# A second Strassen level for four of the seven Q, K and V products, with the sums of x on GpSimd

## The chip, the cores and the metric

The kernel runs on one core of one Trainium2 chip. The metric is the device time of one execution in microseconds (us). The core has five engines with instruction queues of their own: TensorE (PE in the profile, PEld for its weight loads), VectorE (DVE), ScalarE (ACT), GpSimd (POOL) and SyncE (SP), which here only issues DMA transfers. Each queue is worked off in order; engines wait for each other through semaphores.

## The reference, cut to what matters

The program is a small transformer stack on x of shape (8, 512, 1024) in float32. Its first layer is the one that matters here:

```python
qkv = layernorm(x) @ attn_qkvw + attn_qkvb          # (8, 512, 1024) @ (1024, 3072)
q, k, v = split into 32 heads of 32
probs = softmax(q @ k.T / sqrt(32))
ctx = probs @ v
x = x + ctx @ attn_ow + attn_ob                      # (8, 512, 1024) @ (1024, 1024)
```

After it come a dense layer gated by cluster hits, a sigmoid attention, and the dense layer once more. All matrix products are done in float32.

## The kernel before, in words

**Units.** The softmax attention (`softmax_attention`, L421) is a loop over 64 units (L1041). A unit is one batch (of 8) and one group of four heads, 128 columns of Q, K and V. For its four blocks of 128 rows a unit does: scores by rows for the next unit into one PSUM tile `sc` of four banks (`rows_step`, L905), the row maximum by DVE (L906), scores by keys with the maximum subtracted (`keys_step`, L934 and L937, the same single `sc` tile), exp by ScalarE into one of three `pT` buffers (L939), the running sum of `pT` by GpSimd (`sum_step`, L949), and the product with V (`values_step`, L960). `normalize` (L964) divides by the sum and writes `ctxT`.

**Filler.** Everything else that PE has to do is cut into pieces with a weight in us and put into the queue `Filler` (L74). Nine slots of a unit (`between`, L985) each take a share of that queue (`FILLER_SHARES`, L39) between two attention steps. So the order of PE's instructions is written out by hand when the program is built. The pieces come from `project_pieces(n + 2)` (Q, K and V of the unit two ahead), from the output products (`out_products`, L843; `OUT_SHARES` and `LAST_SHARES` say how many of them each unit takes) and from the finished output tiles. All these products go through `product` (L574), so their matmuls are on line L578. Their accumulators are tiles `mm` of one bank from a pool of three (`ps_m`), which the transposes, the denominators and the cluster logits use too.

**Strassen.** From batch 1 on, Q/K and V are computed by one level of Strassen's method in Winograd's form: seven products of half size instead of eight. `LEFT` and `RIGHT` (L139) name the seven operands on the side of x and of the weights. For Q/K of one unit the right-hand columns are Q's and K's, and a product is 4 `product` calls that stream 256 tokens past 128 weight columns. V is done for two units together, with x stationary and 128 weight columns streaming. `gather` (L149) adds each finished product from PSUM into the results: seven DVE adds and two ScalarE copies per set of seven products. `left_sums` (L180) makes the four sums of x of a batch on DVE, 128x1024 each (`left_tasks`, L671). The sums of the weights are made once, on DVE during batch 0, from the weight blocks that batch 0 loads anyway (`sum_weights`, L599), and stored to DRAM by GpSimd's DMA queue. Batch 0 itself uses plain products (`first_pieces`, L617).

**Weights.** A `Stream` (L199) loads weight blocks of 256 KB on SP's queue into six buffers, in the order in which PE will use them (`order`, L464); a block is loaded when the block six before it has been used. The output weights have a stream of their own with six buffers (`OW_BUFS`).

**Small work.** Lists `side` and `slow` hold steps that `between` issues beside the filler: the normalisation of the next batch (`norm_tasks`, L520, its scaling by GpSimd on L558), sums of x, sums of weights.

Of the kernel before, what the change touches and what calls it, by code (L numbers as in the profile page):

```python
# [13 lines left out]
F32 = mybir.dt.float32  # L14
# [8 lines left out]
P = 128  # L23
# [14 lines left out]
W_BUFS, OW_BUFS = 6, 6  # L38
FILLER_SHARES = (0.5, 0.5, 0.6, 1.0, 1.0, 1.0, 0.7, 1.0, 1.0)  # L39

OUT_SHARES = (2, 2, 2, 1)

OUT_SUMS = {0: (0,), 5: (1, 2), 7: (3,)}
LAST_SHARES = {-7: 0, -6: 1, -5: 1, -4: 2, -3: 2, -2: 6, -1: 2}
# [103 lines left out]

def gather(nc, k, acc, ia, ib, ja, jb, bias=(None, None), early=False):  # L149
# [30 lines left out]
def left_sums(nc, a11, a12, a21, a22, s1, s2, s4):  # L180

    tt = nc.vector.tensor_tensor
    steps = [
        partial(tt, s1, a21, a22, ALU.add), partial(tt, s2, s1, a11, ALU.subtract),
        partial(tt, a21, a11, a21, ALU.subtract), partial(tt, s4, a12, s2, ALU.subtract),
    ]
    return dict(A11=a11, A12=a12, A22=a22, S1=s1, S2=s2, S3=a21, S4=s4), steps
# [11 lines left out]
class Stream:  # L199
# [6 lines left out]
    def fill(self, upto):  # L206
        while self.loaded < min(upto, len(self.sources)):
            k = self.loaded
            self.tiles[k] = self.pool.tile(self.shape, F32, tag=self.tag, name=f"{self.tag}_{k}")
            self.nc.sync.dma_start(self.tiles[k], self.sources[k]())  # L210
# [210 lines left out]
def softmax_attention(tc, cst, stage, filler, clusters, pools, dr, late, args):  # L421
# [14 lines left out]
    fixed, ctxp, rpool, npool = outer("a_fixed", 1), outer("a_ctx", 2), outer("a_r", 3), outer("a_n", 1)  # L436
    owpool, csp, xTp, sump = outer("a_ow", OW_BUFS), outer("a_cs", 1), inner("a_xT", 2), inner("a_sum", 1)
    wpool, xpool = inner("a_w", W_BUFS), inner("a_x", 2)
    qkpool, vpool, ptp, tmp = inner("a_qk", 3), inner("a_v", 5), inner("a_pt", 3), inner("a_tmp", 1)
# [9 lines left out]
    xTs, ctxTs, state, lefts = {}, {}, {}, {}  # L449
    units, half = B * NC, NC // 2  # L450

    def quarter(t, g, k):

        return w_view[:, ts(k, half), ts(t * NC + g, P)]

    def weight_source(kind, g, name):

        if name[0] == "T":
            return dr.sums[kind, g, name].rearrange("p (c n) -> p c n", c=half)
        t, g = ((0, g) if name[2] == "1" else (1, g)) if kind == "qk" else (2, 2 * g + int(name[2]) - 1)  # L460
        return quarter(t, g, int(name[1]) - 1)

    V_PARTS = (RIGHT[:4], RIGHT[4:])
    order = []  # L464
    for u in range(NC, units):
        g = u % NC
        order += [("qk", g, RIGHT[k]) for k in EARLY] + [("v", g // 2, name) for name in V_PARTS[g % 2]]
# [11 lines left out]
    used, side, slow, tiles, waiting, ready, held = {"w": 0}, deque(), deque(), deque(), deque(), deque(), []  # L479

    def first_norm():
# [5 lines left out]
        def load(i):  # L487
            pool, tag = (npool, ("n1", "nT")[i % 2]) if i > 1 else (xpool, "x")
# [31 lines left out]
    def norm_tasks(b):  # L520
# [9 lines left out]
        def load(i):  # L530
            st[i] = xpool.tile([P, H], F32, tag="x", name=f"x_{b}_{i}")
# [24 lines left out]
        def apply(k, j):  # L556
# [5 lines left out]
            [partial(load, 0), partial(load, 1)],  # L562
            [partial(turned, k) for k in range(NC // 2)] + [partial(stats, 0), partial(stats, 1)],
            [partial(load, 2), partial(load, 3)],
            [idle] * 3 + [partial(stats, 2), partial(stats, 3)],
            [root, shift, send, idle, spread],
# [13 lines left out]
    first_w = {}  # L580

    def load_first(g, kinds):

        if g >= NC:
            return
        if not first_w:
            first_w["qk"] = ctxp.tile([P, NC, S], F32, tag="ctxT", name="w_first")
        if 2 in kinds:
            wv = rpool.tile([P, H], F32, tag="r", name=f"wv_{g}")
        for t in kinds:  # L590
            for k in range(2):
                at = ts(k, S) if t == 2 else ts((g % 2) * 4 + 2 * t + k, S)
                flat = wv if t == 2 else first_w["qk"].rearrange("p c t -> p (c t)")
                w = first_w[t, g, k] = flat[:, at].rearrange("p (c n) -> p c n", c=half)
                nc.sync.dma_start(w, quarter(t, g, k))
# [1127 lines left out]
```

## Time and profile before

| | |
|---|---|
| runs of the kernel | 3712.62, 3714.6 and 3715.97 us, median 3714.6 |
| the profiled execution | 3715.75 us, span of its instructions 3714.0 us, mean granted clock 0.998 |
| DMA | 598.56 MB, 161 GB/s over the span |
| weight blocks of 256 KB for Q, K and V (`w`) | 252 from the weights, 224 and 112 from stored sums; 2.7 to 3.0 us from issue to landing |
| output weight blocks (`ow`) | 240 from stored sums, 180 from the weights; 3.6 and 3.3 us to landing |

How to read the profile: a row of a group gives line, engine, operation, the tiles written and read, the shapes and the count; then the busy time, the mean duration of one in ns, and the idle time just before them with what ended it. A row of the timeline gives start and duration in us and the number of instructions in the run; durations of matmuls overlap with the next start, so costs are read from start to start. Rows of waits give the total, the number of times and the longest.

### The profile page before, as it was taken

How to read it: one execution, taken by the hardware profiler on the slowest of the kernel's cores; microseconds unless marked ns; L12 is line 12 of the kernel's file. 1: busy time of each engine (PE TensorE's matmuls, PEld its weight loads, DVE VectorE, ACT ScalarE, POOL GpSimd, SP SyncE). 2: the span in 40 equal slices, each digit the busy share in tenths (PEclk: the TensorE clock that was granted, in tenths of full speed). 3: DMA queues.
4: the chain of work that ended last, by engine and by line, in shares of the span. 5: the costliest groups of instructions: out<-in, count | busy, mean ns of one | idle time of the engine just before them, and what ended most of it. 6: DMA issues, size and time to landing. Idle time of an engine off the chain costs nothing.

```text
span 3714.0 us, 76568 instructions
## 1 busy us (share of the span) xinstructions
PE 3677.2 (99%) x32792; PEld 1879.6 (51%) x32792; DVE 2171.2 (58%) x2993; ACT 928.0 (25%) x1017; POOL 1418.9 (38%) x1206
## 2 busy tenths in 40 slices
PE   8999999999999999999999999999999999999999
PEld 4445545545445445455555455534444467774444
DVE  4556555555555555555555555555788845556656
ACT  1222222222222222222222223232111144430000
POOL 2575454454445346345444544442000044530000
PEclk9999999999999999999999999999999999999999
DMA  5345555655655555464565544456566767763332
GB/s 184 106 129 182 143 145 151 183 148 152 185 155 149 169 164 152 143 198 142 149 182 150 151 149 123 122 160 229 158 180 178 184 185 236 222 222 125 133 132 98
DMA packets 728642, 598.56 MB, mean 161 GB/s; under 512 B 322152, under 2 KB 574064, under 8 KB 728304
## 3 DMA queue, kind: packets, MB, share of 16 engines
q1 hardware_dynamic: 701072, 496.40, 47.5%
q0 software_dynamic: 22912, 81.54, 5.6%
q10 hardware_dynamic: 4320, 15.73, 1.0%
q8 instruction: 259, 4.24, 0.5%
q14 instruction: 79, 0.65, 0.1%
HBM read 459.30 MB, written 134.25 MB: 160 GB/s over the span
## 4 chain that ended last, share of the span: by engine, by line
PE 96%; DVE 1%; POOL 1%; issue 1%; DMA 0%; ACT 0%; SPq 0%; POOLq 0%; DVEq 0%; ACTq 0%
PE mm L578 43%; PE dense L1283 21%; PE sc L905 7%; PE av L960 6%; PE sc L937 6%; PE o L1364 4%; PE csc L1345 4%; PE sc L934 2%; PE logitsT L339 2%; PE den L972 1%; PE tp L291 1%; POOL sum L949 0%; PE tpm L578 0%; DMA ow<-o_T 0%; DVE nmax L906 0%
## 5 line engine op out<-in xcount | busy, mean ns | idle before, releaser
L906 DVE TENSOR_REDUCE nmax<-sc 128x4 f32<-128x2048 f32 x256 | 586.5, 2291 | 368.5 <-PE sc L905 365.9
L939 ACT ACTIVATE pT<-sc 128x2048 f32<-128x2048 f32 x256 | 480.7, 1878 | 1113.4 <-PE sc L937 1105.9
L949 POOL TENSOR_TENSOR sum<-sum,pT 128x1024 f32<-128x1024 f32 x256 | 601.1, 2368 | 388.5 <-ACT pT L939 388.4
L949 POOL TENSOR_TENSOR sum<-pT,pT 128x1024 f32<-128x1024 f32 x128 | 309.3, 2438 | 573.9 <-ACT pT L939 547.7
L578 PE MATMUL mm<-xT,w 128*64 128x256 f32 (+1 forms) x3736 | 427.3, 382 | 0.0
L578 PEld LDWEIGHTS mm<-xT,w 128*64 128x64 f32 (+1 forms) x3736 | 241.5, 135 | 202.6 <-issue 44.0
L578 PE MATMUL mm<-s,w 128*32 128x256 f32 (+1 forms) x3672 | 321.0, 381 | 0.0
L905 PE MATMUL sc<-qk,qk 32*64 32x512 f32 x4096 | 285.1, 613 | 0.8 <-ACT pT L939 0.7
L578 PEld LDWEIGHTS mm<-s,w 128*32 128x32 f32 (+1 forms) x3672 | 181.0, 122 | 177.3 <-issue 74.0
L937 PE MATMUL sc<-qk,qk 32*128 32x512 f32 x2048 | 262.9, 587 | 0.0
L156 DVE TENSOR_TENSOR u<-dense,u 128x512 f32<-128x512 f32 x223 | 148.0, 685 | 185.0 <-PE dense L1283 169.6
L578 PE MATMUL mm<-ow,ctxT 128*32 128x512 f32 (+2 forms) x1276 | 249.7, 601 | 2.9 <-DMA ow<-o_T 2.7
L960 PE MATMUL av<-pT,v 128*32 128x512 f32 x2048 | 246.4, 598 | 0.2 <-ACT pT L939 0.2
L1283 PE MATMUL dense<-sum,s 128*128 128x512 f32 x512 | 231.8, 593 | 0.0
L578 PEld LDWEIGHTS mm<-w,xT 128*64 128x64 f32 (+1 forms) x3888 | 197.5, 133 | 62.2 <-issue 48.9
L578 PE MATMUL mm<-w,xT 128*64 128x128 f32 (+1 forms) x3888 | 218.1, 274 | 0.0
L158 DVE SCALAR_TENSOR_TENSOR qk<-mm,qkvb_s,qk 128x256 f32<-128x256 f32 x224 | 107.6, 480 | 155.0 <-PE mm L578 152.3
L156 DVE TENSOR_TENSOR v<-mm,v 128x256 f32<-128x256 f32 x196 | 80.0, 420 | 175.6 <-PE mm L578 174.8
L1283 PE MATMUL dense<-wT_s,dT_b 128*128 128x512 f32 x384 | 171.2, 593 | 0.0
L1283 PE MATMUL dense<-wT_s,dT_a 128*128 128x512 f32 x384 | 171.2, 593 | 0.0
L578 PE MATMUL mm<-ow,c 128*64 128x512 f32 (+2 forms) x864 | 170.0, 596 | 0.3 <-DMA ow<-o_T 0.3
L975 DVE STREAM_TRANSPOSE rden<-den 128x512 f32<-128x512 f32 x64 | 45.9, 717 | 206.6 <-PE den L972 206.6
(236 smaller groups left out, 4772.6 us busy)
## 6 DMA issues: line engine op xcount, KB each, us to landing
w<-in_qkvw SPq DMA_DIRECT2D x252, 256.0 KB, 3.0
ow<-o_T SPq DMA_DIRECT2D x240, 256.0 KB, 3.6
w<-qk_T SPq DMA_DIRECT2D x224, 256.0 KB, 2.8
ow<-in_ow SPq DMA_DIRECT2D x180, 256.0 KB, 3.3
w<-v_T SPq DMA_DIRECT2D x112, 256.0 KB, 2.7
x<-in_x SPq DMA_DIRECT2D x32, 512.0 KB, 4.6
dT_a<-xT SPq DMA_DIRECT2D x32, 512.0 KB, 5.7
x_a<-x SPq DMA_DIRECT2D x32, 512.0 KB, 6.8
```

What stands on the lines that cost most here:

```text
L156: nc.vector.tensor_tensor(out, acc, other, ALU.add)
L158: nc.vector.scalar_tensor_tensor(out, acc, b, other, ALU.add, ALU.add)
L578: nc.tensor.matmul(out[cols], lhsT[:, cols], rhs, **flags)
L905: nc.tensor.matmul(sc[ts(j, P // 2), h, :], st["q"][rows, cols], st["k"][rows, :], start=True, stop=True)
L906: nc.vector.tensor_reduce(st["nmax"][:, qt, :], sc, AX.X, ALU.max, negate=True)
L937: nc.tensor.matmul(sc[:, h, :], st["k"][rows, ts(kt, P)], st["q"][rows, :], start=False, stop=True)
L939: nc.scalar.activation(pT, sc, AF.Exp, scale=SCALE_A)
L949: nc.gpsimd.tensor_tensor(st["sum"][:, h, :], before[:, h, :], st["pT", kt][:, h, :], ALU.add)
L960: nc.tensor.matmul(st["av"][rows, :], st["v"][:, kt, rows], pT[:, h, :], start=(kt == 0), stop=(kt == TPB - 1))
L1283: nc.tensor.matmul(st["acc"], st["left"][LEFT[k]][:, c, :], self.w[RIGHT[k]][:, c, :], start=(c == 0), stop=(c == half - 1),)
L1345: nc.tensor.matmul(sc[:, AT_OFF[i] : AT_OFF[i] + n], k[:, c, ts(i, P)], xT[:, c, i * P :], start=(c == 0), stop=(c == 1),)
L1364: nc.tensor.matmul(acc[:, j - jj, :], at[:, start : start + P], self.v[b * TPB + i][:, cols], start=(i == 0), stop=(i == j),)
```

## The change

Four of the seven products of the first level (the operands numbered 2, 4, 1 and 3 of `LEFT` and `RIGHT`) are themselves done by a second level of the same method. They are taken in pairs, `TWICE = ((2, 4), (1, 3))`; such a pair is called a node here. A node has seven blocks; a block is one weight tile with the operands of both of its products, 4 `product` calls over 128 columns, one accumulator, one `gather`. The three other products ("single" nodes: 0, 5 and 6) stay as they are and are added up by `done`.

- The work is dealt in jobs: Q/K for two units, V for four units. `parts_of` says which part of which job a unit's filler holds: Q/K node pairs in odd units, Q/K singles in even ones; V's first pair when the group's number is 0 modulo 4, the second at 2, the singles at 3. Work for a unit is therefore done up to three units ahead (four at the start of a V job), and starts in unit 4 of batch 0.
- V's single nodes now stream 256 weight columns instead of 128.
- `unit_filler` puts the pieces of output products between the blocks of the doubled nodes; `OUT_SHARES` and `LAST_SHARES` change.
- The sums of x go to GpSimd: per batch four of 1024 elements, four of 512 and eight of 256 (`left_tasks`).
- The sums of weights get a second set of sums (`again`); they load their own operands, and a step of them is issued in each slot with side work, from the scores before unit 0 on. Their results go to DRAM in the block form (`twice`, `once`).
- Batch 0's weights go through the stream too. Pools change: five buffers for Q and K, seven for V, five for output weights, one x buffer; the attention's result lives in six quarter slots (`ctx_s`), with two ScalarE copies at the end (`settle`). The memory for descriptors of GpSimd's DMA queue is set to 4096.

The core of the diff:

```diff
-W_BUFS, OW_BUFS = 6, 6
+W_BUFS, OW_BUFS = 6, 5
+QK_BUFS, V_BUFS, SLOTS = 5, 7, 6
-OUT_SHARES = (2, 2, 2, 1)
+OUT_SHARES = (3, 2, 0, 2)
-LAST_SHARES = {-7: 0, -6: 1, -5: 1, -4: 2, -3: 2, -2: 6, -1: 2}
+LAST_SHARES = {-7: 1, -6: 0, -5: 0, -4: 2, -3: 3, -2: 4, -1: 4}
...
+TWICE = ((2, 4), (1, 3))
+STORED = ("B11", "T3", "B21", "B22", "T1", "T2", "T4")
...
+    def parts_of(u):
+        parts = [("first", u + 2, 0)] if u + 2 < NC else []
+        n = u + 3 if u % 2 else u + 2
+        if NC <= n < units:
+            parts.append(("qk", n, 0 if u % 2 else 1))
+        n = u - u % half + half
+        if n == units:
+            if u % half == 1:
+                parts.append(("v", n - half, 3))
+        elif n >= NC and u % half != 1:
+            last = 4 if n + half < units else 2
+            parts.append(("v", n, (0, None, 1, last)[u % half]))
+        return parts
...
+    def weight_sums(kind, job, c):
...
+        def outer(k):
...
+            st["steps"][k]()
+            if k == 0:
+                once = dr.once[kind, job].rearrange("p (k c n) -> c p k n", k=2, c=2)
+                nc.gpsimd.dma_start(once[c], b11)
+        def again(i, k):
...
+            st["more"][k]()
+            dst = dr.twice[kind, job, i].rearrange("p (m a c n) -> c a p m n", m=7, a=2, c=2)[c]
+            if k == 2:
+                for a in range(2):
+                    nc.gpsimd.dma_start(dst[a, :, 4:], st["z"][:, :, a, :])
+            if k == 3:
+                for a in range(2):
+                    nc.gpsimd.dma_start(dst[a, :, :4], x[:, a].rearrange("p k j n -> p (k j) n"))
...
+        return [load, lambda: None, outers, agains]
...
     def left_tasks(b):
...
+        xT, tt = xTs[b], nc.gpsimd.tensor_tensor
...
+        steps = [
+            partial(tt, e1, b21, b22, ALU.add), partial(tt, e2, e1, b11, ALU.subtract),
+            partial(tt, e3, b11, b21, ALU.subtract), partial(tt, e4, b12, e2, ALU.subtract),
+        ]
...
+        steps += [partial(tt, a21, a11, a21, ALU.subtract), partial(tt, s2, a22, a21, ALU.subtract)]
+        more = [partial(tt, s4, a12, s2, ALU.subtract), partial(tt, s1, s2, a11, ALU.add)]
+        for node, t in ((1, s2), (3, a21)):
...
+            names, own = left_sums(nc.gpsimd, q11, q12, q21, q22, *(e[:, k] for k in range(3)))
...
+        def twice(i, k, at):
+            def go():
...
+                for a in range(2):
+                    for c in range(2):
+                        lhsT, rhs = w[:, a, c, :], left[TWICE[i][a]][k][:, c, :]
+                        if not qk:
+                            lhsT, rhs = rhs, lhsT
+                        product(acc[:, a, :], lhsT, rhs, start=(c == 0), stop=(c == 1))
...
+                gather(nc, k, acc, *(o[j][:, :, m, :] for m in range(2) for j in range(2)), early=True)
+                weights.done(at)
...
+        def done(node, j, acc):
...
+            if node == 0:
+                (ia, ja), (ib, jb) = of(0), of(1)
+                qb = bias(0, j) if qk else None
+                add(ia, acc, qb)
+                add(ib, acc)
+                add(jb, ib)
+                add(ja, jb, qb)
+                return
...
+    def unit_filler(u, products):
+        groups, outs = unit_pieces(u), [piece for product in products for piece in product]
+        many, pieces, at, seen = sum(small for _, small in groups), [], 0, 0
+        for group, small in groups:
+            pieces += group
+            if small:
+                seen += 1
+                upto = len(outs) * seen // many
+                pieces += outs[at:upto]
+                at = upto
+        return weave(pieces, products) if not many else pieces
...
+            if sums:
+                sums.popleft()()
...
-            filler.add(weave(project_pieces(ahead), products), mark=ahead)
...
+        filler.add(unit_filler(n, products), mark=n)
...
-    nc = bacc.Bacc("TRN2", target_bir_lowering=False, num_devices=1)
+    nc = bacc.Bacc("TRN2", target_bir_lowering=False, num_devices=1, dynamic_dma_scratch_size=4096)
```

## The prediction

> **What bounds the kernel now.** I read the page first: its busy times and the chain that ended last. TensorE (PE) is at 99% and the chain is 96% PE. The line to remember is L578, the one matmul line that every projection goes through: 43% of the chain.
>
> ```profile
> PE 3677.2 (99%) x32792; PEld 1879.6 (51%) x32792; DVE 2171.2 (58%) x2993; ACT 928.0 (25%) x1017; POOL 1418.9 (38%) x1206
> PE 96%; DVE 1%; POOL 1%; issue 1%; DMA 0%; ACT 0%; SPq 0%; POOLq 0%; DVEq 0%; ACTq 0%
> ```
>
> An average over the span proves little, so next the busy times by stretch: the 56 units of batches 1 to 7 (second line below), batch 0 before them, the end of the attention after them.
>
> ```profile
> 60.00:277.00 217.00, 215.23 (x2283) 94.44 (x2290) 117.56 (x113) 59.90 (x48) 135.24 (x127) 1.00 0.43 139
> 277.00:2430.00 2153.00, 2150.38 (x25464) 1092.97 (x25455) 1202.37 (x1564) 580.61 (x566) 1019.30 (x722) 1.00 0.54 156
> 2430.00:2600.00 170.00, 157.35 (x1090) 65.35 (x1090) 94.60 (x146) 43.86 (x54) 60.34 (x51) 0.97 0.61 200
> ```
>
> After the time come PE, PEld, DVE, ACT, POOL, then the granted clock, the DMA share and GB/s. In the middle stretch PE idles 2.6 us of 2153 at a granted clock of 1.00, while DVE is at 56%, POOL at 47% and the DMA engines at 54%. So here one us less of PE work is one us less of time, as long as nobody makes PE wait. Only the end has idle PE time (12.7 us).
>
> Third, the timeline of PE gives the price of one `product` (a 128-column stationary operand, issued as two matmuls of 64 columns, each recorded twice: four records).
>
> ```profile
> 1002.63 2.84 PE L578 MATMUL mm<-w,xT 128*64 128x128 f32 x48
> 1005.40 1.11 PE L905 MATMUL sc<-qk,qk 32*64 32x512 f32 x16
> 1006.45 1.95 PE L578 MATMUL mm<-xT,w 128*64 128x256 f32 x16
> 1008.22 0.39 PE L578 MATMUL tpm<-ident_h,parts 128*64 128x128 bf16 x8
> ...
> 1022.70 3.67 PE L578 MATMUL mm<-xT,w 128*64 128x256 f32 x32
> 1026.31 1.11 PE L905 MATMUL sc<-qk,qk 32*64 32x512 f32 x16
> ```
>
> Read from start to start: 12 products over 128 columns take 2.77 us, 0.231 each; 8 over 256 columns take 3.61 us, 0.451 each, and 4 of them 1.77, 0.443 each. Half the columns cost 0.51 of the time, so a second level that halves the moving side does not lose in overhead what it saves.
>
> **What is removed on PE.** Per four units, before: four Q/K groups of 7 x 4 = 28 products over 256 columns (112), and two V jobs of 7 x 8 = 56 over 128 (112). After: each Q/K job of two units has two doubled nodes of 7 blocks x 4 products over 128 columns (56) and three single nodes x 2 columns x 4 over 256 (24); a V job of four units has the same 56 and 24. That is 168 over 128 columns and 72 over 256. Difference: 40 x 0.451 - 56 x 0.231 = 18.0 - 12.9 = 5.1 us per four units, and 14 such groups: 71 us. The attention's own matmuls, the output products and the number of filler slots between them stay, so nothing else moves on PE.
>
> **What is added beside PE.** (a) DVE. Each doubled node gathers as one Strassen level did: 7 adds and 2 ScalarE copies; the three single nodes of a job need the 14 adds that two units need today. Added: 14 adds per Q/K job and 14 per V job, 42 per four units, 588 in all, at the row of L156 (417 to 420 ns): 245 us. The ScalarE copies (372 ns) keep their number. Removed: four sums of x per batch.
>
> ```profile
> L906 DVE TENSOR_REDUCE nmax<-sc 128x4 f32<-128x2048 f32 x256 | 586.5, 2291 | 368.5 <-PE sc L905 365.9 <-PE mm L578 2.5
> L156 DVE TENSOR_TENSOR v<-mm,v 128x256 f32<-128x256 f32 x196 | 80.0, 420 | 175.6 <-PE mm L578 174.8
> L1375 DVE TENSOR_TENSOR s<-xT 128x1024 f32<-128x1024 f32 x7 | 12.5, 1791 | 0.0
> L1375 DVE TENSOR_TENSOR s<-s,xT 128x1024 f32<-128x1024 f32 x7 | 8.6, 1225 | 0.2
> L558 POOL TENSOR_TENSOR xT<-xT,rows 128x1024 f32<-128x1024 f32 x56 | 132.3, 2372 | 0.7
> ```
>
> Those four take 1.79 + 3 x 1.22 = 5.5 us, 38 us over 7 batches. DVE in the middle stretch goes to 1202 + 245 - 38 = 1409 us of some 2082: 68%. It stays under PE, but its bursts grow: a single node 0 ends in four adds (1.7 us), that of V in eight (3.4 us), where one product now ends in two at most.
>
> (b) POOL gets the sums of x: 4 of 1024 elements, 4 of 512 and 8 of 256 a batch. The first at 2.37 us; the others by share of size, 1.2 and 0.6 (an estimate): 19 us a batch, 133 us in all, 1019 to 1152, 55%. They stand ahead of the softmax sums (L949) in POOL's queue, at most 10 us in a unit. Behind these waits the denominator of the next unit, and exp by its three pT buffers. POOL's row of sums is idle 936 us waiting for exp, so the delay is hidden.
>
> (c) Queue of SP: 60 weight blocks of 256 KB per four units instead of 42, 14 x 18 x 256 KB = 66 MB more. At 156 GB/s and a share of 0.54 today that makes about 193 GB/s and 0.67. Six buffers stay. A doubled block lasts 0.9 us on PE, but a unit takes some 37 us for at most 20 of them, so six are 11 us of lead against 2.8 to 3.0 us to landing. SP's own longest row shows the lead: SP waits for PE, not PE for SP. The output weights lose one buffer of six; PE waits 3 us for them now (row "mm<-ow,ctxT"); I add 1 to 4.
>
> ```profile
> SPq L210 <- PE mm L578: 1501.3, 831, 9.1
> PEld mm L578 <- DVE v L156: 44.6, 55, 0.8
> ```
>
> (d) Batch 0. The sums of the weights were 48 adds of 512 elements on DVE (L612, 683 to 908 ns); now 48 of these and 96 of 256, +40 us over nine units of 35 us, at most 3.4 us in one slot and after the row maximum of that slot in the queue; hidden as long as DVE (54% here) has them done before the next maximum, a slot pair of 7 us later. POOL issues 108 stores instead of 48. Its rows are 0.55 us for a plain store and 1.07 us for the one finely cut load (L1405), so +33 to +90 us on a POOL at 62%: up to 9 us a unit. SP's loads for these sums wait for the stores that read the same buffers (landing 4 to 5 us), and weight blocks are queued behind those loads. Cost: 0 to 15 us; no row shows a POOL store with the smaller descriptor memory, so above that lies the case where each issue waits for the landing before (108 x 4.4 us). I take 5.
>
> (e) Work is projected up to three units ahead, so some of the last units' filler moves into batch 0. The last two units get 4 + 4 output products instead of 6 + 2. The idle PE time of 12.7 us lies there; two copies of 128x1024 at 1.23 us (settle) join it. -8 to +8, I take -3.
>
> (f) Waits for the three accumulators. A doubled block fills one in 0.9 us where a single product took 1.8. If two blocks follow the row maximum (2.29 us) and the next slots want the first one's accumulator, PE waits for 2.29 + 0.42 us from the end of the scores. Slots are three pieces or 2.6 us, then keys (1.2 us): mostly covered; in slot one of a unit the first block goes to ScalarE, which is free. The wait row above (weight loads that wait for DVE, 55 times at up to 0.8 us, PE not idle) says that cover is already thin. One wait of 0.5 us in a unit is 28 us, none is 0; I take 8.
>
> **A rule against it.** DVE's first sum of x takes 1791 ns where its like takes 1225, beside POOL's scaling of x. The Trainium skill, "SBUF — State Buffer", section "Who interferes with whom", says that a DVE instruction with two SBUF inputs and a GpSimd one that reads SBUF exclude each other, the later one blocking fully. The change puts more such work on POOL. By it the 168 adds of node 0 with both inputs in SBUF would each wait up to one POOL sum, half of that time on average: by estimate some 1.2 us x 0.55 x 168 = 111 us of DVE, a share of 73%. By the row alone (0.57 us) it is 96 us at the most. Either way the forecast stands.
>
> **The sum.** -71 (PE) + 8 (accumulators) + 2 (output weights) + 5 (batch 0) - 3 (end) = -59. The profiled execution took 3715.75 us (span 3714.0), the median is 3714.6, 1.15 below: 3715.75 - 59 - 1.15 = 3655.6, say 3655.
>
> **Rivals.**
> 1. Forecast: PE's saving stands, waits take 0 to 30 us of it: 3640 to 3675. 0.70. Better than that, with the end filled as well: 3630 to 3640, 0.05.
> 2. Waits eat half: accumulators at 0.5 us a unit (28), batch 0 at 15 more, late blocks in the units where 14 doubled blocks and 12 output blocks meet (6.8 MB in 37 us are 184 GB/s, and some 220 with the rest, which is 156 today less 119 for 17.5 such blocks a unit). 3715 - 71 + 30 to 62: 3675 to 3706. For: the thin cover. Against: PE's zero idle. 0.12.
> 3. Slower, one mechanism: DVE's queue in front of the row maximum. The score buffer is single, so scores, maximum (2.29), keys and exp (1.88) go round in turn, and filler covers the maximum by only some 0.3 us. If the bursts make it late in each of the four rounds of a unit by s, PE loses 56 x 4 x s: it decides from s = 0.32 us (71 / 224). At 0.5 us: 112 - 71 = +41, 3755. For: four-add bursts of 1.7 us against scores of 1.05 us. Against: only the last accumulator before a scores slot counts, and 68% is no full engine. 0.10.
> 4. It does not save what it says: 128-column products in small groups cost more than 0.231, break-even at 18.0 / 56 = 0.32 us. The run of 12 above, which spans more than one accumulator, speaks against it. 3708 to 3722, 0.03.
>
> **Numbers.** Range 3636 to 3698: case 1 nearly whole, and three quarters of case 2; left out are the slower cases and the tails. Faster by over 0.2% (below 3707; about what a measurement of this kernel can tell from no change): 0.87. Within 0.2%: 0.03. Slower: 0.10.
>
> **What would show it.** In the profile after: four units take about 152 us instead of 157; L578 over 256 columns falls by a third and over 128 columns rises by a half; PE idle stays under 10 us in the middle stretch; DVE near 68%, POOL near 55%, DMA share near 0.65. Wrong if PE waits at L934 or L905 for DVE nmax (case 3), at L578 for DMA w (case 2), or if PE idles in batch 0 beside POOL.

## The result, and the profile after

The changed kernel takes 3897.9 us (median of 4 runs, 3895.9 to 3910.6) against 3715.3 for the one before: ratio 1.050, 95% interval 1.0475 to 1.0523. It is 5% slower, where the forecast was 1.6% faster. The profiled execution took 3899.2 us, with a span of 3897.5.

The page of after, busy times and the chain that ended last:

```profile
PE 3675.3 (94%) x34228; PEld 1929.0 (49%) x34228; DVE 2569.3 (66%) x3649; ACT 940.5 (24%) x1047; POOL 1634.9 (42%) x1378
PE 79%; DVE 12%; DMA 4%; issue 2%; POOL 2%; ACT 1%; SPq 0%; DVEq 0%; ACTq 0%; POOLq 0%
```

PE was 96% of the chain and is 79%; DVE has 12% of it and DMA 4%. PE stopped being the only bound. The stretches (columns as in the prediction): batch 0 and batches 1 to 6 of the kernel before, then batch 0, batches 1 to 6 and the last units of after.

```profile
60.00:347.00 287.00, 283.58 (x3163) 130.81 (x3164) 165.36 (x167) 79.61 (x65) 174.67 (x162) 1.00 0.44 141
347.00:2229.00 1882.00, 1881.85 (x22146) 954.03 (x22144) 1049.26 (x1376) 503.12 (x491) 898.33 (x628) 1.00 0.55 160
```

```profile
60.00:420.00 360.00, 319.88 (x3654) 162.92 (x3656) 232.94 (x309) 81.95 (x72) 247.43 (x232) 0.95 0.66 199
420.00:2411.00 1991.00, 1865.03 (x23336) 988.97 (x23338) 1358.94 (x1857) 513.44 (x516) 1044.33 (x734) 0.98 0.63 180
2411.00:2660.00 249.00, 228.71 (x2740) 106.63 (x2735) 156.24 (x206) 71.25 (x67) 111.97 (x84) 0.99 0.47 137
```

In the middle stretch PE is idle for 1991 - 1865 = 126 us, where it had none, and its granted clock is 0.98 instead of 1.00. No engine is full: DVE is at 68%, POOL at 52%, the DMA engines at 0.63, all three about as forecast. Measured between starts of units (a unit starts here where its transposed maxima `tpm` begin; idle time from 60 us on, in pieces of over 0.15 us):

| us | start to unit 8 | units 8 to 55 | units 56 to 62 | rest |
|---|---|---|---|---|
| before | 347.2 | 1882.2 | 263.6 | 1221.0 |
| after | 420.8 | 1990.0 | 246.2 | 1240.5 |
| PE idle before / after | 3 / 40 | 0 / 125 | 5 / 19 | 12 / 21 |

About 21 us of work moved from the end into batch 0 (by the trace of `p12` below, where PE hardly waits there: 305 us of PE work against 284). The rest of the +73.6 there is lost, and in the middle the losses are larger than the +107.8, since PE's saving lies there too. What PE waited for in after (total us, times, longest):

```profile
PE sc L1126 <- DVE nmax L1098: 91.8, 67, 5.2
PE mm L647 <- DMA w<-in_qkvw: 26.3, 13, 5.1
PE mm L647 <- issue: 13.1, 5, 2.6
PE tpm L647 <- POOL parts L1108: 12.9, 26, 3.0
```

The first row is rival 3's: the row maximum is late. A piece of the timeline of after shows why:

```profile
1302.15 5.25 POOL L1141 TENSOR_TENSOR sum<-pT,pT 128x1024 f32<-128x1024 f32 x2 [0.26 <-ACT pT L1131]
...
1302.75 1.11 PE L1097 MATMUL sc<-qk,qk 32*64 32x512 f32 x16
1302.97 2.15 DVE L975 TENSOR_TENSOR c<-ctx_s 128x512 f32<-128x512 f32 x1
1305.04 0.41 DVE L163 TENSOR_TENSOR qk<-mm,qk 128x256 f32<-128x256 f32 x1
1305.38 2.58 DVE L975 TENSOR_TENSOR c<-c,ctx_s 128x512 f32<-128x512 f32 x1
...
1307.88 2.28 DVE L1098 TENSOR_REDUCE nmax<-sc 128x4 f32<-128x2048 f32 x1
...
1310.21 0.40 PE L1126 MATMUL sc<-shift,ones_h 32*128 32x512 bf16 x4 [2.71 <-DVE nmax L1098]
```

PE's scores end at 1303.9. DVE is then inside an add of two SBUF tiles that lasts 2.15 us; later comes another of 2.58, both beside GpSimd's softmax sums. Undisturbed they take 0.68. The add between them, with PSUM as one input, takes its usual 0.41. The maximum starts 4.0 us late and PE waits 2.7 us. From here on, time that such an add loses beside GpSimd is called a hold-off. The adds of the output products in both kernels, before first, then after; below them two rows of after for adds of node 0, which the kernel before doesn't have:

```profile
L769 DVE TENSOR_TENSOR r<-r,ob_s 128x1024 f32<-128x1024 f32 x30 | 38.7, 1291 | 7.4 <-DMA r<-in_x 7.4
L788 DVE TENSOR_TENSOR r<-ct,r 128x512 f32<-128x512 f32 x45 | 29.8, 690 | 1.0
```

```profile
L959 DVE TENSOR_TENSOR r<-r,ob_s 128x1024 f32<-128x1024 f32 x30 | 60.5, 2017 | 0.0
L978 DVE TENSOR_TENSOR r<-ct,r 128x512 f32<-128x512 f32 x45 | 51.5, 1171 | 1.0
L844 DVE SCALAR_TENSOR_TENSOR qk<-qk,qkvb_s,qk 128x256 f32<-128x256 f32 x56 | 51.0, 911 | 2.0
L842 DVE TENSOR_TENSOR qk<-qk 128x256 f32<-128x256 f32 x56 | 43.8, 782 | 1.9
```

The first two have the same number and shapes in both kernels and 1.6 to 1.7 times the duration. Over all of DVE, time above the usual duration of the same form (its fastest tenth), called the excess below, rose from some 50 to some 250 us. Counted in the traces, 1 of the 45 `r<-ct,r` begins during one of GpSimd's softmax sums before, 26 of 45 after. In after these 26 take 1529 ns on average and the 19 others 682. The adds from PSUM into Q, K and V that begin during a softmax sum, 313 of them, take at most 485 ns, their usual duration.

### The profile page after: what moved, and what is told of

Same layout as the page of the kernel before. It is cut to its first block, busy times and chain, and to the rows that moved or that the text cites. A ratio compares the mean times of both kernels' runs of the same rounds, so it can differ in the third digit from the quotient of the medians.

```text
span 3897.5 us, 81316 instructions
## 1 busy us (share of the span) xinstructions
PE 3675.3 (94%) x34228; PEld 1929.0 (49%) x34228; DVE 2569.3 (66%) x3649; ACT 940.5 (24%) x1047; POOL 1634.9 (42%) x1378
## 4 chain that ended last, share of the span: by engine, by line
PE 79%; DVE 12%; DMA 4%; issue 2%; POOL 2%; ACT 1%; SPq 0%; DVEq 0%; ACTq 0%; POOLq 0%
PE mm L647 31%; PE dense L1496 20%; PE av L1152 6%; PE sc L1129 5%; PE sc L1097 5%; DVE nmax L1098 4%; PE o L1577 3%; PE csc L1558 3%; PE sc L1126 2%; DMA w<-in_qkvw 2%; DVE r L978 1%; PE logitsT L349 1%; PE den L1191 1%; DVE qk L842 1%; DVE r L959 1%
## 5 line engine op out<-in xcount | busy, mean ns | idle before, releaser
L1141 POOL TENSOR_TENSOR sum<-sum,pT 128x1024 f32<-128x1024 f32 x256 | 613.2, 2417 | 332.9 <-ACT pT L1131 332.8
L647 PE MATMUL mm<-xT,w 128*64 128x128 f32 (+6 forms) x4164 | 390.8, 344 | 22.6 <-DMA w<-in_qkvw 20.1
L647 PEld LDWEIGHTS mm<-xT,w 128*64 128x64 f32 (+2 forms) x4164 | 229.2, 132 | 188.2 <-issue 112.2
L647 PE MATMUL mm<-s,w 128*64 128x256 f32 (+3 forms) x3288 | 288.1, 351 | 25.8 <-issue 13.1
L647 PE MATMUL mm<-ow,ctx_s 128*64 128x512 f32 (+2 forms) x1168 | 262.3, 600 | 4.4 <-DMA ow<-o_T 3.9
L647 PEld LDWEIGHTS mm<-s,w 128*64 128x64 f32 (+1 forms) x3288 | 175.5, 129 | 179.9 <-issue 68.0
L647 PEld LDWEIGHTS mm<-e,w 128*64 128x64 f32 (+1 forms) x3456 | 178.6, 134 | 84.8 <-issue 41.6
L647 PE MATMUL mm<-e,w 128*64 128x128 f32 (+1 forms) x3456 | 206.5, 278 | 11.8 <-DVE qk L163 6.5
L163 DVE TENSOR_TENSOR qk<-mm,qk 128x256 f32<-128x256 f32 x392 | 157.9, 417 | 80.2 <-PE mm L647 72.9
L647 PE MATMUL mm<-w,xT 128*64 128x128 f32 (+4 forms) x2816 | 194.0, 296 | 3.7 <-DMA w<-t_v 3.7
L1126 PE MATMUL sc<-shift,ones_h 32*128 32x512 bf16 x1024 | 102.8, 390 | 98.7 <-DVE nmax L1098 91.8
L647 PEld LDWEIGHTS mm<-w,xT 128*64 128x64 f32 (+2 forms) x2816 | 150.8, 133 | 63.3 <-issue 29.3
L647 PE MATMUL mm<-ow,c 128*64 128x512 f32 (+2 forms) x816 | 178.2, 597 | 2.1 <-DMA ow<-o_T 2.1
```

The source lines that it names most:

```text
L163: nc.vector.tensor_tensor(out, acc, other, ALU.add)
L647: nc.tensor.matmul(out[cols], lhsT[:, cols], rhs, **flags)
L1126: nc.tensor.matmul(sc[:, h, :], cst.ones_h[rows, :], st["shift"][rows, :], start=True, stop=False)
L1141: nc.gpsimd.tensor_tensor(st["sum"][:, h, :], before[:, h, :], st["pT", kt][:, h, :], ALU.add)
```

## Experiments

The theory after this comparison: DVE's adds with two SBUF inputs are held off by GpSimd's reads of SBUF (the exclusion, or port theory, of the expectations) and make the row maximum late; weight blocks are late at the turn of a batch; the weight sums disturb batch 0. Rivals: DVE simply has more to do, 66 MB more of weights, the move of the sums of x to GpSimd. All but `p9` are single executions beside a run of the kernel before (3714 to 3717 us). The four executions of after spread over 15 us, so a difference of that size in one run alone says little without its trace.

**1. GpSimd's softmax sums filled with ones** (`p1`).

```diff
-            nc.gpsimd.tensor_tensor(st["sum"][:, h, :], before[:, h, :], st["pT", kt][:, h, :], ALU.add)
+            nc.gpsimd.memset(st["sum"][:, h, :], 1.0)
```

> Edit: GpSimd's softmax sums (L1141) become plain fills of the sum tile with 1.0, so they write SBUF and read nothing; the softmax denominators are left out of the computation. Port theory (DVE instructions with two SBUF inputs wait behind GpSimd instructions that read SBUF, which makes the row maximum late): the rows r<-r,ob_s, r<-ct,r, qk<-qk and c<-c,ctx_s go back from 2017, 1171, 782 and about 2000 ns to some 1224, 690, 420 and 690; PE's wait for DVE nmax falls from 92 us to under 20; the time from 3898 to 3750 to 3815. Load theory (588 more adds make DVE's queue too long by themselves): nothing changes, 3885 to 3905. Weight theory (PE waits for late weight blocks): 3885 to 3905, the waits for DMA w stay near 30 us.

Measured: 3785.5 us. DVE's excess falls from 250 to 95 us, waits for the maximum to 32 us (under 20 were expected), waits for weight blocks stay (22.5). The time is what the exclusion expects; but the fill also takes away the sums' wait for exp and is shorter than a sum, so experiments 8 and 9 follow.

**2. The same sums in instructions of half the size, and of a quarter** (`p2`, 512 elements, shown; `p8`, 256, with `range(2 * GH)`).

```diff
-        for h in (slice(0, GH // 2), slice(GH // 2, GH)):
+        for h in range(GH):
```

> Edit: each GpSimd softmax sum is cut from two instructions of 1024 elements (2.4 us) into four of 512 (some 1.25 us); same work and result, GpSimd a little busier. Port theory: a blocked DVE instruction waits for at most 1.25 us instead of 2.4, so the wait for nmax falls from 92 us to 30 to 60 and the time to 3820 to 3870. Load theory: 3890 to 3910, nothing gained.

> The kernel after, with GpSimd's softmax sums in eight instructions of 256 elements in place of two of 1024. Theory of the exclusion (a DVE instruction waits for the GpSimd instruction that runs): the longest wait falls from 2.4 to some 0.7 us, so more is won than with quarters of 512 (3845.6 us): 3805 to 3838 us, with GpSimd's own time up by less than 150 us. Theory that it is GpSimd's total reading time that counts: no better than quarters, 3845 to 3900 us.

Measured: 3845.6 and 3847.6 us. Halving gives 52 us. The second halving gives nothing in all: 4.5 us in the middle stretch, lost again in batch 0 and at the end, while GpSimd's sums grow from 1009 to 1134 us. The first expectation is met in time (the waits for the maximum are 62 us, just above it), the second is a miss for the exclusion in its simple form (only the length of one GpSimd instruction counts). The single hold-off does shrink: adds with two SBUF inputs that begin during a softmax sum run over by 1.2, 0.6 and 0.4 us on average in after, `p2` and `p8`. What no longer follows is the time.

**3. Fewer adds on DVE** (`p3`).

```diff
-                gather(nc, k, acc, ...)
+                if k in (0, 3, 4):
+                    gather(nc, k, acc, ...)
```

> Edit: of the seven gathers of a doubled node only three are done (k 0, 3, 4), so 420 of the 588 added DVE adds are left out (Q, K and V are wrong). They read one operand from PSUM, so none of them has two SBUF inputs. Load theory: DVE back to about its share of before, the wait for nmax under 20 us, 3760 to 3800. Port theory: the two-SBUF rows keep their long durations (2017, 1171, 911 ns), the wait for nmax stays over 50 us, 3830 to 3880, a part of the gain because an idle queue forgives a blocked instruction.

Measured: 3815.3 us, between the two. 420 adds that all read PSUM, and are never held off themselves, are worth 83 us, though `r<-ct,r` still takes 1172 ns. So plain load in front of the maximum counts too: the queue is what PE waits for, whoever fills it. How the two share, the traces tell by an estimate: for each wait, add up the hold-offs in DVE's unbroken run of work ahead of the maximum. In the middle stretch of after they cover 57.7 of the 59.0 us of waits, and in `p3` 26.6 of 27.5. So there the load uses up the cover, and nearly every wait needs a hold-off on top.

**4. The sums of x back on DVE, and to GpSimd in the kernel before** (`p4`, `p5`).

```diff
-        xT, tt = xTs[b], nc.gpsimd.tensor_tensor
+        xT, tt = xTs[b], nc.vector.tensor_tensor
...
-            names, own = left_sums(nc.gpsimd, q11, q12, q21, q22, *(e[:, k] for k in range(3)))
+            names, own = left_sums(nc.vector, q11, q12, q21, q22, *(e[:, k] for k in range(3)))
```

and in the kernel before

```diff
-def left_sums(nc, a11, a12, a21, a22, s1, s2, s4):
-
-    tt = nc.vector.tensor_tensor
+def left_sums(nc, a11, a12, a21, a22, s1, s2, s4, engine=None):
+
+    tt = (engine or nc.vector).tensor_tensor
...
-        lefts[b], steps = left_sums(nc, a11, a12, a21, a22, *sums)
+        lefts[b], steps = left_sums(nc, a11, a12, a21, a22, *sums, engine=nc.gpsimd)
```

> Edit: only the sums of x go back from GpSimd to DVE (16 instructions a batch). Theory that this move is the cause: 3740 to 3790. Port theory with the softmax sums as the main blocker (939 of GpSimd's reading time against 133 for the sums of x): the sums of x now have two SBUF inputs on DVE themselves and block there; the wait for nmax stays at 60 to 120 us, 3860 to 3930.

> The kernel before, with its four sums of x per batch on GpSimd and nothing else changed. If the exclusion of DVE and GpSimd costs time only where DVE has more to do ahead of the row maximum than the cover holds, the kernel before has room for it: 3710 to 3722 us, PE idle in batches 1 to 6 under 5 us. If more GpSimd reads alone are enough to make the row maximum late, 3735 to 3790 us.

Measured: 3924.0 and 3717.0 us. The move is not the cause; undone, it costs 26 us, and in the kernel before it costs nothing.

**5. The normalization's rows in packets of 32 bytes** (`p6`).

```diff
-            nc.sync.dma_start(dr.rows[b].rearrange("(k t p) -> p k t", k=2, p=P), st["rows"])
+            nc.sync.dma_start(dr.rows[b].rearrange("(p k t) -> p k t", p=P, k=2), st["rows"])
...
```

The part left out lets GpSimd read the rows back in that order.

> The kernel after, with the rows of the normalization sent in 128 packets of 32 bytes in place of 1024 packets of 4, and read back in that order by GpSimd. Theory that the weight blocks are late because the 4-byte packets hold up the DMA engines: PE's 26 us of waits for weight blocks in batches 1 to 6 fall under 8, with some of the half clock behind them; 3850 to 3880 us. Theory that they are late because 66 MB more of weights are loaded: nothing changes, 3890 to 3905 us.

What it was made for, in the windows of after at a turn of batches (the last figure is GB/s):

```profile
1400.00:1405.00 5.00, 3.98 (x40) 2.86 (x48) 0.27 (x1) 1.00 (x1) 3.92 (x2) 1.00 0.98 163
1405.00:1410.00 5.00, 2.91 (x40) 1.67 (x24) 4.42 (x7) 0.58 (x1) 0.74 (x1) 1.00 0.72 35
1410.00:1415.00 5.00, 4.29 (x28) 2.50 (x28) 0.75 (x2) 0.00 (x0) 0.00 (x0) 0.66 0.69 160
```

With the 4-byte store in flight the engines are busy (0.72) and move 35 GB/s, PE runs dry for 2.1 us of five, and then runs at a clock of 0.66. The issue of one more load lasts 6.59 us on SP's queue, which holds up the weight loads behind it too:

```profile
1405.14 6.59 SPq L605 DMA_DIRECT2D xT<-in_xT  x1
```

Measured with 32 bytes: 3881.0 us, 1 us above the expected range; the store lands in 1.4 to 5.1 us instead of 12.2 to 14.3, no issue on L605 lasts over 2.2 us (7.6 in after), and waits for `w<-in_qkvw` in the middle stretch fall from 26 to 4 us. That the store makes the blocks late is shown; whether by the engines or by SP's queue is not. Only 17 us reach the end. In the same run the waits for the maximum rise from 91.8 to 109.5 us (GpSimd's scaling of x, now with strided rows, goes from 2.4 to 2.9 us), which may account for the rest. The kernel before has the same store, landing in 11.3 to 13.2 us, and no wait for these blocks; experiment 11 shows what has to come together.

**6. Batch 0's weight sums** dealt finer (`p7`), without their adds (`p10`), left out (`p11`).

```diff
-        return [load, lambda: None, outers, agains]
+        return [load, lambda: None, lambda: None] + outers + agains
...
-            if sums:
-                sums.popleft()()
+        if sums:
+            sums.popleft()()
```

```diff
-            st["steps"][k]()
...
-            st["more"][k]()
...
```

```diff
...
-    sums = deque(step for job in jobs for c in range(2) for step in weight_sums(*job, c))
+    sums = deque(lambda: None for _ in range(50))
...
```

In `p10` and `p11` the parts left out let stores and products take plain blocks of the weights, in packets of the same size.

> The kernel after, with the weight sums of batch 0 dealt over nine places of a unit in place of five and the four outer sums in two steps, so that at most four sums stand in front of a row maximum at once. Theory that bursts of sums on DVE make batch 0 long: the stretch up to unit 8 falls from 421 to 390 to 408 us, the whole to 3868 to 3888 us. Theory that the stores of GpSimd and the loads behind them on SP's queue make it long: the stretch stays at 415 to 430 us, the whole at 3890 to 3910 us.

> The kernel after with the weight sums' adds on DVE left out (144 instructions of batch 0); what is loaded and stored keeps its sizes and order, the stores take loaded halves of the weights instead, so the products of three of the seven blocks use wrong weights. Theory that DVE's part makes batch 0 long: the stretch up to unit 8 falls from 421 to 375 to 392 us. Theory that the loads on SP's queue wait for GpSimd's stores, and the weight blocks behind them: the stretch stays above 405 us.

> The kernel after with the weight sums of batch 0 left out altogether: no loads, adds or stores for them; the products that need sums take plain blocks of the weights in packets of the same size, so Q, K and V of batches 1 to 7 are wrong. By the comparison of the traces batch 0 lost 74 us, 21 of it work that came from the end of the attention: the stretch up to unit 8 falls from 421 to 360 to 378 us, the whole to 3837 to 3858 us. If batch 0 is long because more pieces of unit 8 to 10 are computed in it, the stretch stays above 400 us.

Measured up to unit 8: 420.1, 381.7 and 369.6 us (after: 420.8); in all 3887.9, 3844.5 and 3833.7. The sums cost 51 us in batch 0, 39 of it their adds on DVE, 12 the loads and stores. Dealing them finer wins nothing there, so it is not the bursts but the amount (and the hold-off, up to 2.6 us for an add of 0.42). The expectation on bursts was a miss.

**7. All three causes out at once, and the best whole version** (`p12`: the edits of `p1`, `p6` and `p11`; `p9`: those of `p8`, `p6` and `p7`).

> The kernel after with all three suspected causes taken away at once: GpSimd's softmax sums become a fill with ones (the denominators are left out), the rows go in packets of 32 bytes, and the weight sums of batch 0 are left out as above (wrong Q, K and V). If PE's saving of 71 us is there and only these three ate it: 3645 to 3695 us, below the kernel before. If the saving does not exist, or a fourth wait eats it: 3710 to 3750 us.

> The kernel after with the three changes tried singly so far: softmax sums in eighths (-50 us alone), the rows sent in packets of 32 bytes (-17), the weight sums spread (-10). If their gains add up: 3821, say 3805 to 3840 us, and so still slower than before. If the same cover is counted twice (a maximum that is late anyway hides a late weight block), 3840 to 3850 us. Faster than before (under 3707) by neither theory.

`p12` takes 3696.2 us, 1 us above the upper edge of what was expected. Its page and its three stretches:

```profile
PE 3620.8 (98%) x34228; PEld 1899.5 (51%) x34228; DVE 2322.0 (63%) x3505; ACT 939.9 (25%) x1047; POOL 986.8 (27%) x1270
```

```profile
60.00:370.00 310.00, 305.42 (x3675) 153.49 (x3674) 146.66 (x182) 82.34 (x73) 108.01 (x135) 1.00 0.42 132
370.00:2219.00 1849.00, 1829.64 (x23318) 970.44 (x23316) 1214.05 (x1845) 512.31 (x515) 607.57 (x723) 1.00 0.64 191
2219.00:2460.00 241.00, 227.98 (x2732) 105.87 (x2729) 145.16 (x206) 71.41 (x67) 50.59 (x83) 0.99 0.48 140
```

The clock is back at 1.00, PE's idle time in the middle at 19 us, the stretch at 1849 against 1882. So the saving exists, and these three took 3898 - 3696 = 202 us. `p12` leaves out work that the kernel before does as well, but there PE idles 3 us in batch 0 and 0 in the middle, so it has little to win by that (not run). Singly the three are 112 (experiment 1), 17 (5) and 64 (6), 193 in all. `p9` keeps the whole computation (sums in instructions of 256, rows of 32 bytes, finer weight sums): 3840.2 us, ratio 1.033, interval 1.0317 to 1.0352. It lies on the border of the two expectations: the single gains are 77 us, together they are 58, as if some cover had been counted twice.

**8. As many adds, but one input in PSUM** (`p13`).

```diff
-                add(jb, ib)
-                add(ja, jb, qb)
+                add(jb, acc)
+                add(ja, acc, qb)
```

and `r<-ct,r` likewise.

> The kernel after with the two-SBUF-input adds of node 0 (168) and of the output products (45) reading the accumulator in PSUM in place of their first SBUF input: as many adds of the same size, but Q, K, V and the output projection are wrong. They carry some 80 of the 250 us by which DVE's instructions run over. Theory of the exclusion: the row maximum's 92 us of waits fall by a third or more, with some of the half clock: 3820 to 3870 us. Theory that DVE's load counts: nothing changes, 3885 to 3905 us.

Measured: 3847.8 us, in the range of the exclusion; the waits for the maximum fall from 91.8 to 67.2 us, less than the third that was expected. The adds of L842, L844 and L978 that had two SBUF inputs are now part of these rows of `p13`:

```profile
L844 DVE SCALAR_TENSOR_TENSOR qk<-mm,qkvb_s,qk 128x256 f32<-128x256 f32 x224 | 106.3, 476 | 95.0 <-PE mm L647 94.1 <-PE tpm L647 0.6
L978 DVE TENSOR_TENSOR r<-mm,r 128x512 f32<-128x512 f32 x135 | 90.0, 685 | 110.3 <-PE mm L647 103.5 <-ACT ct L984 6.9
L842 DVE TENSOR_TENSOR qk<-mm,qk 128x256 f32<-128x256 f32 x168 | 65.1, 416 | 0.0
```

911, 1171 and 782 ns have become 476, 685 and 416, and 50 us of time are gone, at the same number of instructions. Load alone can't do that: the second SBUF input is what is held off. The Trainium skill, "SBUF — State Buffer", section "Who interferes with whom", says this (a pair of ports shared by DVE and GpSimd, held exclusively), and these rows agree; that only GpSimd's reads exclude, not its writes, it says too, and `p1` agrees (next experiment).

**9. GpSimd reads constants** (`p15`).

```diff
...
-            nc.gpsimd.tensor_tensor(st["sum"][:, h, :], before[:, h, :], st["pT", kt][:, h, :], ALU.add)
...
+            nc.gpsimd.tensor_tensor(out, ones, ones, ALU.add)
```

> The kernel after with GpSimd's softmax sums reading two constant tiles of ones in place of exp's results (the denominators are left out): as many instructions of the same size that read SBUF, but no wait for exp. Theory of the exclusion: little is won against 3898, 3865 to 3910 us, and DVE's excess over its usual durations stays above 200 us. Theory that the sums' hold on exp's buffers is the cause: like the fill with ones, 3780 to 3800 us.

Measured: 3884.0 us, DVE's excess 218 us. With the reads left (1935 ns each instead of 2417) and the wait for exp gone, 14 us are won (32 in the middle stretch, of which batch 0 loses 15 again); with the reads gone as well, 112. A fill is also shorter than such an add, so look at single adds, first in `p1`, then in `p15`:

```profile
2388.35 1.84 POOL L1141 MEMSET sum<- 128x1024 f32 x2
2389.70 0.43 DVE L842 TENSOR_TENSOR qk<-qk 128x256 f32<-128x256 f32 x1
```

```profile
519.76 4.10 POOL L1143 TENSOR_TENSOR sum<-ones 128x1024 f32<-128x1024 f32 x2 [1.68 <-PE den L1193]
520.11 2.00 DVE L844 SCALAR_TENSOR_TENSOR qk<-qk,qkvb_s,qk 128x256 f32<-128x256 f32 x1
```

All 14 adds with two SBUF inputs that begin during a fill in `p1` keep their usual duration. In `p15` the 8 adds of L844 that begin during an add of constants take 1997 or 1998 ns instead of 485 and end 0.3 us after GpSimd's instruction. It is the reads; the two-input adds that still run over in `p1` begin beside GpSimd's other adds, the sums and the scaling of x.

**10. The two-input adds on GpSimd** (`p14`, on top of `p9`).

```diff
-                add(jb, ib)
+                nc.gpsimd.tensor_tensor(jb, ib, jb, ALU.add)
...
```

The other add of node 0, the bias of the output rows and the context sums of the output products move to GpSimd too, and the bias of node 0 to ScalarE.

> The kernel with the three changes (3840 us) and, on GpSimd in place of DVE, the two-SBUF-input adds of node 0 (their bias goes to ScalarE), the bias of the output rows and the sums of the context for the output products. Theory of the exclusion: DVE is hardly held off in batches 1 to 6, the row maximum's waits there fall from 34 to under 10 us: 3790 to 3825 us. Theory that GpSimd's queue becomes the next wait (node 5's adds and the output products then wait for it): 3840 to 3900 us.

Measured: 3927.4 us, beyond both. DVE is held off less (excess some 140 us, 215 in `p9`), but the maximum's split (`parts`) waits in GpSimd's queue:

```profile
PE sc L1127 <- ACT shift L1119: 62.3, 25, 8.8
PE tpm L649 <- POOL parts L1109: 49.8, 31, 4.3
PE sc L1127 <- DVE nmax L1099: 40.6, 48, 5.3
```

**11. The place of the output products** (`p16` four blocks later, `p17` dealt 2, 2, 2, 1 as before, `p18` the former on `p9`).

```diff
-                upto = len(outs) * seen // many
+                upto = len(outs) * max(seen - 4, 0) // (many - 4)
```

```diff
-OUT_SHARES = (3, 2, 0, 2)
+OUT_SHARES = (2, 2, 2, 1)
```

> The kernel after with the output products of a unit starting four blocks later in its filler. In the trace of after the context sums (c<-) of a unit lie 12 to 20 us behind its start, on GpSimd's softmax sums; in before they lie at 21 to 27 us, between two pairs of those sums. Theory that the place decides: the context sums' means (1.3 to 2.1 us) fall under 1.1 us, and the whole to 3850 to 3882 us. Theory that the amount of GpSimd's reads decides: the means stay, 3888 to 3908 us.

> The kernel after with the output products dealt over four units as before, 2, 2, 2 and 1 in place of 3, 2, 0 and 2. Theory that the place decides: the means of the output products' adds (r<-ct,r 1171, r<-r,ob_s 2017, context sums 1327 to 2119 ns) change by more than a fifth in one direction or the other, and the time follows their sum, 3840 to 3885 us if fewer of them meet a softmax sum. Theory of the amount: means and time stay, 3888 to 3908 us.

> The kernel with the three changes (3840 us) and the output products four blocks later. If the place decides and the softmax sums in eighths have not already taken its gain: 3810 to 3832 us. If they have: 3833 to 3850 us.

Measured: 3904.5, 3854.5 and 3905.8 us. In `p16` the place does what was said to the adds (context sums from 1327, 1846 and 2119 to 743, 834 and 681 ns, though the fourth sum goes from 678 to 1622; `r<-ct,r` from 1171 to 775) and DVE's excess falls from 250 to 180 us, yet no time is won: the waits for the maximum are fewer and longer (52 times 84.5 us in all), beside more half clock (79 us in the middle stretch). Of the 51.5 us of these waits in the middle stretch, hold-offs cover only 28.7. So it seems that crowding the products at the end of the unit makes its own queue. In `p17` `r<-ct,r` grows to 1672 ns and the time still falls by 43 us: waits for `w<-in_qkvw` are gone from the longest rows, and the maximum's fall to 79.5 us. So the place decides who is held off, but the time doesn't follow the sum of the hold-offs. The late blocks of after lie almost all in unit 7 of a batch and at the start of the next unit. By the shares 3, 2, 0, 2 that unit 7 takes no output product, so its 20 weight blocks follow each other without one in between; by 2, 2, 2, 1 it takes two. In `p17` the store of experiment 5 still takes 10.4 to 11.6 us to land, and no wait for `w<-in_qkvw` is left. By these runs it takes the store and the unit without output products together. `p18` is a miss, and why it loses 66 us against `p9` is open.

## Why the prediction was wrong

**The step that failed** is "A rule against it". The rule was found and priced as busy time of DVE for the 168 adds of node 0 (111 us, "a share of 73%"), and then "Either way the forecast stands": it entered the sum with nothing. DVE's share was no question (68%, as forecast). What counts is where the time falls: in front of a maximum whose cover the same text had put at 0.3 us, where it made 59 us of waits in the middle stretch, with half clock behind them. And the rule holds for every add with two SBUF inputs. Node 0's run over by 57 us; those of the output products by 95 us, 4 in the kernel before, though the change adds none of them but only moves them onto GpSimd's sums. The trace of before could have shown it: 690 ns, 1 of 45 meeting a sum, though GpSimd works 48% of that time. Such a number comes from the order of the work, and the change redid that order. The row that the step did read, the first sum of x with 1791 ns, was misread: all seven of them begin during a softmax sum on L949, not during the scaling of x. It was thus the softmax sums, over 900 us of GpSimd's time, that had to be counted. That the sums of x on GpSimd delay nothing, as (b) had it, was right (`p4`, `p5`).

**Rival 3** was the mechanism, with 0.10 and a price of 3755. Its burst of node 0 is part of it; it had left out the hold-offs. In batches 1 to 6 the waits come to 59 us over 48 units of four rounds, 0.31 us a round, near the 0.32 at which it put the loss of the whole saving. The rest came by other ways.

**PE, -71.** `p12` has 784 products over 128 columns more and 560 over 256 less than before, just as counted. From start to start the latter save 252 us (253 forecast); the former cost 192 (181 forecast), since a 128-column product takes 0.235 us on average and not 0.231. So -60.

**(c) output weights, 2, late weight blocks, nothing, and DMA at 0.67.** The share was right (0.63), and PE's waits for output weights went from 3 to 6 us. The lead of six buffers held too, but for the turn of a batch, where a store of 4-byte packets meets a unit without output products: 26 us of waits. Rival 2 had late blocks, but in the units with the most output products. For the shares of the output products, which `p17` shows to be worth 43 us, the sum had no term.

**(d) batch 0, 5, between 0 and 15.** Measured 51. The loads and stores, on which the step dwelt, are 12 of it. The 96 added sums, "hidden as long as DVE has them done before the next maximum", are presumably most of another 39 (for all 144 sums, of which the kernel before had 48): they were not done in time.

**(e) the end, -3.** The last units are 17 us shorter and the rest is 19 longer, although 21 us of work moved into batch 0: the end lost some 23 us, about as much as PE's idle time there grew (17 to 40).

**(f) accumulators, 8.** The rows of L647 that wait for DVE `qk` (9.5 and 7.6 us) are this, partly again behind adds that were held off. The row "issue" (13.1, five waits of 2.6) may be; the profile names nobody.

**Not in any step: the clock.** Behind most gaps of 2 us and more comes a piece at half clock; see the last section.

Together: -60 (PE), +185 (PE's idle time: 205 us in the four stretches against 20), and half of the 108 us more at half clock, 54: +179, where the spans differ by 183. Load (`p3`) and hold-off (`p13`) don't add up, since nearly every wait in the middle stretch needs both; in batch 0 and at the end, where hold-offs cover 18 of 33 us of the waits for the maximum, the rest stays open. A version that beats the kernel before was not found; `p9` with the shares of `p17` was not tried.

## What to carry to other kernels

Where a trace shows an engine at half load and nobody waiting for it, ask whether that is slack or the luck of an order: count how many of its instructions with two SBUF inputs begin while GpSimd adds, and expect the free count to be lost when the order is redone. Price a hold-off at the place where it lies (in front of which instruction, with how much cover), not as a share of an engine. And look for small stores of few bytes near loads that have little lead.

## What the runs showed of the hardware

- A DVE add of 128x512 with two SBUF inputs that begins during a GpSimd add takes up to 2.9 us instead of 0.68; with one input in PSUM it keeps its duration (L978: 685 against 1171 ns). A GpSimd fill (no reads, 960 ns) doesn't hold it off: 14 of 14 adds in `p1` kept theirs.
- After gaps in PE's work the granted clock is 0.50 for 3.41 us, or twice that: 64.8 us in the middle stretch of after, 34.1 in batch 0, none in the same stretches of before; in the middle stretch of `p12`, with 19 us of idle time in small pieces, none again. From batch 0 to the last units of after, each of the 26 such pieces begins at a gap of 1.9 us or more or within 3.5 us behind it, and 26 of the 36 gaps of that length have one. In them PE's matmuls over 128 columns start 107 ns apart instead of 55. So, by an estimate, one late maximum can cost 1.7 us more than its gap, half of 3.41, and at times twice that.
- A store of 1024 packets of 4 bytes lands in 12 to 14 us; with it in flight, for some 8 us of the piece shown in experiment 5, only 24 to 40 GB/s move (35 with the DMA engines 0.72 busy). As 128 packets of 32 bytes it lands in 1.4 to 5.1 us.
